# The top-k threshold of three batches found bit by bit with sign passes, in place of rounds of the eight largest

## The chip, the core and the metric

The kernel runs on one NeuronCore of a Trainium2 chip. The metric is the device time of one execution, in microseconds (us). Engines are named as the profile names them: PE is the matrix engine (its weight loads stand apart as PEld), DVE the vector engine, ACT the scalar engine, POOL the GpSimd engine, SP the engine that issues most DMAs. Each engine works through its own queue in order, and an instruction may wait for semaphores that other instructions, of other engines or of its own, count up.

## The reference, cut to what matters

The model has four steps, each added to the residual `x` (4 batches of 512 tokens of 512 numbers): a learned adjacency, a quantized feed-forward with Hadamard transforms, a 16-head cross attention over latent context, and a second quantized feed-forward. Only the first is changed:

```python
x = x + tanh(g_xattn[0]) * adjacency(ctx_512, layernorm(x), Wq, Wk, gamma_raw)

def adjacency(h, adj_raw, Wq, Wk, gamma_raw):       # h: 4 x 512 x 128
    ...                                             # Q, K: four heads of h @ Wq.T, h @ Wk.T
    sim = einsum('bhnd,bhmd->bnm', Q, K) / (sqrt(32.0) * 4)       # 4 x 512 x 512
    k = 153                                         # 0.3 of 512
    threshold = top_k(sim, k)[0][:, :, -1:]         # of each row: its 153rd largest
    A = sigmoid(sim) * (sim >= threshold)
    A = (A + swapaxes(A, -1, -2)) * 0.5
    gamma = sigmoid(gamma_raw)
    return (1 - gamma) * adj_raw + gamma * A
```

So each of the 512 rows of similarities of a batch needs its own threshold, the 153rd largest of its 512 numbers.

## The kernel before, in words

**Tiles.** The 512 rows of a batch lie as NT = 4 tiles of 128 partitions by 512 numbers, all in fp32. `adjacency(b)` projects the context (PE, tile `pq`), forms the similarities of each tile with one matmul into PSUM (`psim`, line 475) and copies them scaled to SBUF with ACT (`sim`, line 477). Then come `rounds` = 20 rounds for two tiles at a time: DVE's MAX8 finds the eight largest of each row (`m`, line 486), and MATCH_REPLACE8 overwrites these eight with -3e38 in a work tile (`work`, line 491; the hardware runs it as a short MATCH_VALUE_LOAD and the pass itself). After round 20 the wanted number is the first of the last eight. A pass of DVE (line 497) then keeps the sigmoid (ACT, line 496) where the similarity is at least this threshold. Transposes on PE (`padj`) and three passes on DVE add it to `x`. For batch 0 all this runs alone, at the start of the kernel.

**Staging.** For batches 1 to 3, the adjacency, then the keys of the attention (`keys(b)`), then the first feed-forward (`feed0`) of batch b are generators that run in the background of the attention of batch b-1. `attention` loops over 32 pairs of heads, eight for a batch, and over four steps j within a pair. In each step it emits the current pair's scores and the next pair's queries:

- `pqh` (line 804): queries by PE, copied by ACT (`qh`, line 809); `pb` (819): queries through the compressed weights; DVE multiplies by cosines and sines (`ro`, `rs`, lines 827 to 832); POOL adds (833); `pr` (790, 792), copied by ACT (`qr`, 850).
- `pss` (863, 866): scores by PE; DVE takes the negated maximum of a row (`nm`, 871); ACT computes the exponentials with their sum (`pp`, 874, with an ACTIVATION_READ_ACCUMULATOR behind each), DVE the reciprocal (`rsm`, 876), ACT the scaled probabilities (877).
- `ppt` (885): transposes by PE, copied by ACT (`pT`, 886).
- at the pair's end `pc` (893): attended context by PE, copied by ACT (`cxo`, 898); `po` (905): output projection; DVE adds it to `x` (910).

**What sets the order.** The loop at the end of the kernel calls `next` on the attention, then draws on a background generator as long as the costs that it has yielded lie under a budget: a budget of 230 is spread over the steps up to four before batch b's attention begins, and what is left then is emitted at once. A tile framework puts the instructions of each engine in order and sets the semaphores. The DVE rounds of the top-k carry a lowered priority (`high_priority(offset=-FILL)`), so they fill the queue behind the attention's own work. With other work in flight, `gate_t` hands out one of two 2 KB buffers, `front_t` one of three, and `big` one of three 8 KB buffers.

Of the kernel before, what the change touches and what calls it, by code (L numbers as in the profile page):

```python
# [9 lines left out]
F32 = mybir.dt.float32  # L10
BF = mybir.dt.bfloat16
AF = mybir.ActivationFunctionType
ALU = mybir.AluOpType
AX = mybir.AxisListType

P = 128
B, S, D = 4, 512, 512
NT = S // P
# [6 lines left out]
TOPK = max(1, int(S * 0.3))  # L25
SIM_SCALE = 1.0 / (math.sqrt(32.0) * 4.0)
EPS = 1e-5
MAGIC = 12582912.0
GONE = -3.0e38
U16 = mybir.dt.uint16  # L30
F8 = mybir.dt.float8e4


# [1 line left out]
def flamingo_kernel(  # L35
# [9 lines left out]
    nc = tc.nc  # L45

    const = ctx.enter_context(tc.tile_pool(name="const", bufs=1))
    small = ctx.enter_context(tc.tile_pool(name="small", bufs=4))
    xp = ctx.enter_context(tc.tile_pool(name="xp", bufs=8))
# [16 lines left out]
    alone = [True]  # L66
    turn_of = {"tr": 0, "big": 0, "front": 0}

    def mine(kind, every):
        turn_of[kind] += 1  # L70
        return not alone[0] or turn_of[kind] % every == 0

    def bg_ps(name):
        return psb.tile([P, 512], F32, tag="bg", name=name)

    def gate_ps(name):
        return mm_ps(name) if alone[0] else bg_ps(name)
# [6 lines left out]
    def two_k(tag, bufs, name):  # L84
        return bp.tile([P, 512], F32, tag=tag, name=name, bufs=bufs)

    def front_t(name):
        if mine("front", 2):
            return two_k("front", 3, name)
        return wp.tile([P, 512], F32, tag="pp", name=name, bufs=7)  # L90

    def gate_t(name):
        if alone[0]:
            return wp.tile([P, 512], F32, tag="ro", name=name, bufs=7)
        return two_k("gate", 2, name)

    def back_t(name):
        return two_k("back", 2, name)
# [3 lines left out]
    def big(name):  # L102
        place = lent.pop(0) if lent else None
        if place == "h":
            t = hp.tile([P, NC, S], F32, tag="hT", name=name, bufs=1)
            return t.rearrange("p c s -> p (c s)")
        if place == "t":
            t = wp.tile([P, NT, S], F32, tag="pT", name=name)
            return t.rearrange("p j s -> p (j s)")
        if place == "b":  # L110
            return bp.tile([P, FF], F32, tag="big", name=name, bufs=3)
        turn_of["big"] += 1
        if not alone[0] or turn_of["big"] % 5 in (1, 3, 0):
            return bp.tile([P, FF], F32, tag="big", name=name, bufs=3)
        t = wp.tile([P, NT, S], F32, tag="pT", name=name)
        return t.rearrange("p j s -> p (j s)")
# [56 lines left out]
    def ln_stats(tiles, name):  # L173

        k = len(tiles)
        st = small.tile([P, k, 6], F32, tag=f"ln_st{k}", name=f"st_{name}")
        mv = small.tile([P, k, 2], F32, tag=f"ln_mv{k}", name=f"mv_{name}")
        for j, t in enumerate(tiles):
            nc.vector.bn_stats(st[:, j, :], t)
            nc.vector.bn_aggr(mv[:, j, :], st[:, j, :])  # L180
        return mv, rsqrt_cols(mv[:, :, 1], k, name)
# [261 lines left out]
    xs = {}  # L443

    FILL = 800

    def adjacency(b):
        cT = front_t(f"cT_{b}")
        nc.sync.dma_start(cT, cxT[:, b * S : (b + 1) * S])
        proj = []  # L450
        for i in range(2):
            pq = bg_ps(f"pq_{b}_{i}")
            nc.tensor.matmul(pq, wqk[:, i, :], cT, start=True, stop=True)
            t = bp.tile([P, S], F32, tag=f"qk{i}", name=f"qk{i}_{b}")
            nc.scalar.copy(t, pq)
            proj.append(t)
        qT, kT = proj
        if alone[0]:
            adj = hp.tile([P, NT, S], F32, tag="hT", name=f"adj_{b}", bufs=1)
        else:  # L460
            adj = big(f"adj_{b}").rearrange("p (j s) -> p j s", j=NT)
        rounds = (TOPK + 7) // 8
        at = (TOPK - 1) % 8
        for two in range(0, NT, 2):
            if two == (0 if alone[0] else NT - 2):
                for k in range(NT):
                    t = xp.tile([P, D], F32, tag="x", name=f"x{b}_{k}")
                    nc.sync.dma_start(t, x[(b * NT + k) * P : (b * NT + k + 1) * P, :])
                    xs[b, k] = t
            pair = range(two, two + 2)  # L470
            sims, works, m8 = {}, {}, {}
            for j in pair:
                i = f"{b}_{j}"
                psim = bg_ps(f"psim_{i}")
                nc.tensor.matmul(psim, qT[:, j * P : (j + 1) * P], kT, start=True, stop=True)
                sims[j] = gate_t(f"sim_{i}")
                nc.scalar.activation(sims[j], psim, AF.Copy, scale=SIM_SCALE)
                works[j] = back_t(f"work_{i}")


            cur = dict(sims)
            for r in range(rounds):
                with tc.high_priority(offset=-FILL):
                    for j in pair:
                        m8[j] = small.tile([P, 8], F32, tag="m8", name=f"m8_{b}_{j}_{r}")
                        nc.vector.max(m8[j], cur[j])  # L486
                yield 1.3
                with tc.high_priority(offset=-FILL):
                    if r < rounds - 1:
                        for j in pair:  # L490
                            nc.vector.match_replace(works[j], m8[j], cur[j], GONE)  # L491
                            cur[j] = works[j]
                yield 1.4
            for j in pair:
                sg = front_t(f"sig_{b}_{j}")
                nc.scalar.activation(sg, sims[j], AF.Sigmoid)
                nc.vector.scalar_tensor_tensor(
                    adj[:, j, :], sims[j], m8[j][:, at : at + 1], sg, ALU.is_ge, ALU.mult
                )
        mv, r = ln_stats([xs[b, j] for j in range(NT)], f"a{b}")  # L500

        kr = small.tile([P, NT], F32, tag="ckr", name=f"ckr_{b}")
        nc.vector.tensor_scalar(kr, r, c_keep, None, ALU.mult)
        km = small.tile([P, NT], F32, tag="ckm", name=f"ckm_{b}")
        nc.vector.scalar_tensor_tensor(km, mv[:, :, 0], -1.0, kr, ALU.mult, ALU.mult)
        nc.vector.tensor_scalar(kr, kr, 1.0, None, ALU.add)
        yield 5.0
        for j in range(NT):
            i = f"{b}_{j}"
            pt = gate_ps(f"padj_{i}").rearrange("p (k q) -> p k q", k=NT)  # L510
            for k in range(NT):
                nc.tensor.transpose(pt[:, k, :], adj[:, k, j * P : (j + 1) * P], ident)
            if alone[0]:
                nc.scalar.activation(
                    xs[b, j], xs[b, j], AF.Identity, bias=km[:, j : j + 1], scale=kr[:, j : j + 1]
                )
            else:
                nc.vector.tensor_scalar(
                    xs[b, j], xs[b, j], kr[:, j : j + 1], km[:, j : j + 1], ALU.mult, ALU.add
                )  # L520
            sym = front_t(f"sym_{i}")
            nc.vector.tensor_tensor(sym, adj[:, j, :], pt.rearrange("p k q -> p (k q)"), ALU.add)
            nc.vector.scalar_tensor_tensor(
                xs[b, j], sym, c_new, xs[b, j], ALU.mult, ALU.add
            )
            yield 2.0
# [433 lines left out]
    def step(gen, parts):  # L960
        for _ in range(parts):
            next(gen, None)

    a0, early, fw = adjacency(0), ahead(), feed_weights(True, "w0")
    step(early, 1)
    w0 = None
# [36 lines left out]
    def before(b):  # L1003
        k = keys(b)
        for n, cost in enumerate(adjacency(b)):
            yield cost
            if n % 6 == 5:

                with tc.high_priority(offset=-FILL // 4):
                    step(k, 1)  # L1010
        drain(k)
        yield from feed0(b, w0)
# [16 lines left out]
    for _ in attention(first):  # L1029
        done += 1  # L1030
        while job < len(jobs):
            gen, cost, until = jobs[job]
            start = jobs[job - 1][2] if job else 0
# [145 lines left out]
```

## Time and profile before

| what | value |
|---|---|
| time, median of 3 runs | 2048.83 us (2048.23 to 2052.68) |
| the profiled execution: time | 2048.82 us, all of it the span from the first to the last instruction |
| PE busy | 1819.6 us, 89% of the span |
| DVE busy | 1630.3 us, 80% |
| ACT busy | 1081.8 us, 53% |
| POOL busy | 336.1 us, 16% |
| MAX8, lines 486, all four batches | 320 instructions, 209.5 us of DVE |
| attention, first `pc` to last `po` | 312 us to 1961 us of the span |

The page gives, for each engine, the busy time, its course in 40 slices of 51 us, and groups of instructions with their mean duration and the idle time before them. Two instructions that follow each other on one engine overlap a little in the trace: the second starts before the first's end. So what an instruction takes of its engine is read from one start to the next start, and not from its duration. The stage of a background step can be read from windows of the trace that run from one pair's first `pc` matmul to the next pair's.

### The profile page before, as it was taken

How to read it: one execution, taken by the hardware profiler on the slowest of the kernel's cores; microseconds unless marked ns; L12 is line 12 of the kernel's file. 1: busy time of each engine (PE TensorE's matmuls, PEld its weight loads, DVE VectorE, ACT ScalarE, POOL GpSimd, SP SyncE). 2: the span in 40 equal slices, each digit the busy share in tenths (PEclk: the TensorE clock that was granted, in tenths of full speed). 3: DMA queues.
4: the chain of work that ended last, by engine and by line, in shares of the span. 5: the costliest groups of instructions: out<-in, count | busy, mean ns of one | idle time of the engine just before them, and what ended most of it. 6: DMA issues, size and time to landing. Idle time of an engine off the chain costs nothing. (4 is left out here: it accounts for less than half of the span.)

```text
span 2048.8 us, 22947 instructions
## 1 busy us (share of the span) xinstructions
PE 1819.6 (89%) x7874; PEld 889.2 (43%) x7874; DVE 1630.3 (80%) x3305; ACT 1081.8 (53%) x1833; POOL 336.1 (16%) x316
## 2 busy tenths in 40 slices
PE   1268799999999999999999999999989999999898
PEld 0035534436554344455444444555443444444333
DVE  7989699987776999977778999778758556866785
ACT  6935454354434455453444564534786565555544
POOL 3020031123011122130111221301111210111000
PEclk6579899999999999999999999999999999999999
DMA  7451021111111222111122121111783112222011
GB/s 269 155 179 38 1 74 45 55 49 28 42 43 48 89 71 72 38 38 37 41 55 84 57 84 47 35 35 38 241 302 128 50 40 74 68 53 67 21 34 39
DMA packets 115556, 151.90 MB, mean 74 GB/s; under 512 B 57456, under 2 KB 68080, under 8 KB 112368
## 3 DMA queue, kind: packets, MB, share of 16 engines
q1 hardware_dynamic: 109968, 134.51, 22.0%
q0 software_dynamic: 4320, 14.16, 1.9%
q10 hardware_dynamic: 1152, 1.77, 0.2%
q8 instruction: 62, 1.02, 0.2%
q14 instruction: 54, 0.44, 0.1%
HBM read 117.90 MB, written 19.92 MB: 67 GB/s over the span
## 5 line engine op out<-in xcount | busy, mean ns | idle before, releaser
L833 POOL TENSOR_TENSOR ro<-ro,rs 128x512 f32<-128x512 f32 x192 | 255.4, 1333 | 1153.3 <-DVE rs L829 648.3
L874 ACT ACTIVATE pp<-pss,nm 128x512 f32<-128x512 f32 x256 | 174.6, 685 | 272.3 <-DVE nm L871 271.5
L804 PE MATMUL pqh<-hT,wq 128*128 128x512 f32 x512 | 239.7, 606 | 6.8 <-ACT pp L874 5.6
L893 PE MATMUL pc<-pT,kv 128*128 128x512 f32 x512 | 236.0, 600 | 2.7 <-ACT pT L886 2.6
L905 PE MATMUL po<-om,cxo 128*128 128x512 f32 x512 | 229.9, 597 | 0.0
L819 PE MATMUL pb<-qh,wc 128*128 128x512 f32 x384 | 189.4, 613 | 13.6 <-ACT qh L809 7.7
L486 DVE MAX8 m<-work 128x8 f32<-128x512 f32 x304 | 198.7, 684 | 0.6
L871 DVE TENSOR_REDUCE nm<-pss 128x1 f32<-128x512 f32 x256 | 167.8, 683 | 38.1 <-PE pss L866 37.9
L491 DVE MATCH_REPLACE8 work<-m,work 128x512 f32<-128x512 f32 x288 | 193.6, 678 | 0.1
L877 ACT ACTIVATE pp<-pp,rsm 128x512 f32<-128x512 f32 x256 | 178.6, 720 | 27.4 <-DVE rsm L876 26.2
L886 ACT COPY pT<-ppt 128x512 f32<-128x512 f32 x256 | 142.1, 588 | 38.5 <-PE ppt L885 38.0
L885 PEld LDWEIGHTS ppt<-ident,pp 128*128 128x128 f32 x1024 | 117.7, 142 | 96.6 <-issue 37.1
L885 PE MATMUL ppt<-ident,pp 128*128 128x128 f32 x1024 | 147.8, 279 | 10.1 <-ACT pp L877 4.4
L910 DVE SCALAR_TENSOR_TENSOR x<-po,gt,x 128x512 f32<-128x512 f32 x128 | 94.8, 745 | 68.4 <-PE po L905 67.6
L804 PEld LDWEIGHTS pqh<-hT,wq 128*128 128x128 f32 x512 | 93.1, 191 | 128.4 <-issue 89.6
L863 PE MATMUL pss<-kr,qr 64*128 64x512 f32 x256 | 143.4, 641 | 4.4 <-ACT pp L874 2.6
L905 PEld LDWEIGHTS po<-om,cxo 128*128 128x128 f32 x512 | 93.9, 190 | 119.5 <-issue 101.2
L866 PE MATMUL pss<-kr,qr 64*128 64x512 f32 x256 | 143.4, 641 | 0.7 <-DVE ro L827 0.5
L827 DVE TENSOR_TENSOR ro<-pb,cos_q 128x512 f32<-128x512 f32 x192 | 130.9, 682 | 10.3 <-PE pb L819 9.5
L893 PEld LDWEIGHTS pc<-pT,kv 128*128 128x128 f32 x512 | 91.9, 190 | 105.0 <-issue 90.4
L819 PEld LDWEIGHTS pb<-qh,wc 128*128 128x128 f32 x384 | 65.6, 189 | 113.6 <-issue 40.9
L898 ACT COPY cxo<-pc 128x512 f32<-128x512 f32 x64 | 37.4, 584 | 145.1 <-PE pc L893 144.8
(279 smaller groups left out, 3062.0 us busy)
## 6 DMA issues: line engine op xcount, KB each, us to landing
wq<-in_wqh SPq DMA_DIRECT2D x64, 256.0 KB, 2.7
om<-omd SPq DMA_DIRECT2D x64, 256.0 KB, 2.8
wc<-in_wkcq SPq DMA_DIRECT2D x32, 384.0 KB, 3.1
krd<-krs POOLq DMA_DIRECT2D x32, 256.0 KB, 2.5
kr<-krd SPq DMA_DIRECT2D x32, 256.0 KB, 2.7
sa_w1v<-in_gvT SPq DMA_DIRECT2D x8, 1024.0 KB, 5.3
sb_w1v<-in_gvT SPq DMA_DIRECT2D x8, 1024.0 KB, 5.2
wr<-in_wqr SPq DMA_DIRECT2D x32, 192.0 KB, 2.4
```

The lines of the kernel that those rows point to most:

```text
L486: nc.vector.max(m8[j], cur[j])
L491: nc.vector.match_replace(works[j], m8[j], cur[j], GONE)
L804: nc.tensor.matmul(pq, self.wqs[i][:, c, :], hT[self.b][:, c, :], start=(c == 0), stop=(c == NC - 1),)
L819: nc.tensor.matmul(pb, self.wc[:, at : at + P], self.qhs[i if i < 2 else o], start=True, stop=True)
L833: nc.gpsimd.tensor_tensor(ro, ro, rs, ALU.add)
L863: nc.tensor.matmul(*args, start=True, stop=True)
L871: nc.vector.tensor_reduce(nm, pss[i], AX.X, ALU.max, negate=True)
L874: nc.scalar.activation(pp, pss[i], AF.Exp, bias=nm, accum_out=sm)
L877: nc.scalar.activation(pp, pp, AF.Copy, scale=rs)
L885: nc.tensor.transpose(pt[:, l, :], pp[:, l * P : (l + 1) * P], ident)
L893: nc.tensor.matmul(pc, kv[self.b][:, l, :], self.pT[i][:, l, :], start=(l == 0), stop=(l == NT - 1),)
L905: nc.tensor.matmul(po, self.cxo[i][:, j * P : (j + 1) * P], self.oms[i], start=(i == 0), stop=(i == 1),)
```

## The change

For batches 1 to 3 the rounds go. All four similarity tiles are copied to the 8 KB buffer `adj` first; then `kth` finds the 153rd largest of each row. It settles one bit of the fp32 pattern at a time: a first pass finds the sign of the wanted number, and each of 31 further steps tests a candidate. The count of the numbers above the candidate comes from ACT: a Sign activation of `sig * sim + test` with a running sum along the row, one pass for each of the four tiles, into one column of `cnt` each. The sign tiles themselves go to one scratch buffer, `junk`. Then three DVE operations on 128 x 4 numbers compare the counts with `need` and set and clear bits of `test`. At the end some small DVE operations and one counting pass of DVE for each tile settle the last bit. Sigmoid and masking stay as they were. Batch 0 keeps its rounds.

```diff
+    def kth(b, sims):
+        st = small.tile([P, 8, NT], F32, tag="kth", name=f"kth_{b}", bufs=1)
+        cnt, sig, need, test, r, u, hi, lo = (st[:, k, :] for k in range(8))
+        ints = lambda t: t.bitcast(I32)
+        junk = gate_t(f"signs_{b}")
+
+        def signs(**how):
+            for j in range(NT):
+                col = slice(j, j + 1)
+                nc.scalar.activation(
+                    junk, sims[:, j, :], AF.Sign, accum_out=cnt[:, col],
+                    **{k: v[:, col] for k, v in how.items()},
+                )
+
+        nc.vector.memset(test, -2.0)
+        signs()
+        nc.vector.tensor_scalar(sig, cnt, float(2 * TOPK - S), 2.0, ALU.is_ge, ALU.mult)
+        nc.vector.tensor_scalar(sig, sig, 1.0, None, ALU.subtract)
+        nc.vector.tensor_scalar(need, sig, float(2 * TOPK - S - 1), 1.0, ALU.mult, ALU.add)
+        yield 3.4
+        for bit in range(30, -1, -1):
+            signs(scale=sig, bias=test)
+            nc.vector.tensor_tensor(ints(r), cnt, need, ALU.is_lt)
+            if bit:
+                nc.vector.tensor_scalar(
+                    ints(r), ints(r), bit, 1 << (bit - 1), ALU.logical_shift_left, ALU.bitwise_or
+                )
+            nc.vector.tensor_tensor(ints(test), ints(test), ints(r), ALU.bitwise_xor)
+            yield 3.4
...
+        for j in range(NT):
+            nc.vector.tensor_scalar(
+                junk, sims[:, j, :], hi[:, j : j + 1], 0.0, ALU.is_ge, ALU.add,
+                accum_out=cnt[:, j : j + 1],
+            )
+        nc.vector.tensor_scalar(ints(u), cnt, float(TOPK), None, ALU.is_ge)
+        nc.vector.copy_predicated(lo, ints(u), hi)
+        yield 5.0
+        return lo
+
     def adjacency(b):
...
+        if not alone[0]:
+            for j in range(NT):
+                psim = bg_ps(f"psim_{b}_{j}")
+                nc.tensor.matmul(psim, qT[:, j * P : (j + 1) * P], kT, start=True, stop=True)
+                nc.scalar.activation(adj[:, j, :], psim, AF.Copy, scale=SIM_SCALE)
+                yield 1.0
+            limit = yield from kth(b, adj)
+            tokens()
+            for j in range(NT):
+                sg = front_t(f"sig_{b}_{j}")
+                nc.scalar.activation(sg, adj[:, j, :], AF.Sigmoid)
+                nc.vector.scalar_tensor_tensor(
+                    adj[:, j, :], adj[:, j, :], limit[:, j : j + 1], sg, ALU.is_ge, ALU.mult
+                )
-        for two in range(0, NT, 2):
+        for two in range(0, NT if alone[0] else 0, 2):
...
```

`tokens()` is the loading of the batch's four tiles of `x`, which stood between the two pairs of tiles before and now follows `kth`. The sign passes have no lowered priority.

More of the change, by code (lines that the diff above doesn't have):

```diff
@@ L29 @@
 GONE = -3.0e38
-U16 = mybir.dt.uint16
+I32 = mybir.dt.int32
 F8 = mybir.dt.float8e4
@@ L445, in flamingo_kernel @@
     FILL = 800
+    def kth(b, sims):
[25 more added lines that the diff above has]
+            yield 3.4
+        nc.vector.tensor_scalar(ints(test), ints(test), 0x7FFFFFFF, None, ALU.bitwise_and)
+        nc.vector.memset(ints(u), 1)
+        nc.vector.tensor_tensor(ints(r), ints(test), ints(u), ALU.add)
+        nc.vector.tensor_scalar(ints(u), sig, 0.0, None, ALU.is_gt)
+        nc.vector.tensor_copy(hi, test)
+        nc.vector.tensor_copy(lo, r)
+        nc.vector.copy_predicated(hi, ints(u), r)
+        nc.vector.copy_predicated(lo, ints(u), test)
+        nc.vector.tensor_tensor(hi, hi, sig, ALU.mult)
+        nc.vector.tensor_tensor(lo, lo, sig, ALU.mult)
+        for j in range(NT):
[7 more added lines that the diff above has]
+        return lo
     def adjacency(b):
@@ L463, in adjacency, with tokens @@
         at = (TOPK - 1) % 8
-        for two in range(0, NT, 2):
[L465 to L469, printed above, removed]
+        def tokens():
+            for k in range(NT):
+                t = xp.tile([P, D], F32, tag="x", name=f"x{b}_{k}")
+                nc.sync.dma_start(t, x[(b * NT + k) * P : (b * NT + k + 1) * P, :])
+                xs[b, k] = t
+        if not alone[0]:
[13 more added lines that the diff above has]
+        for two in range(0, NT if alone[0] else 0, 2):
+            if two == 0:
+                tokens()
             pair = range(two, two + 2)
```

## The prediction

> **What bounds the kernel now.** I read the page first: its busy times, then its slices.
>
> ```profile
> PE 1819.6 (89%) x7874; PEld 889.2 (43%) x7874; DVE 1630.3 (80%) x3305; ACT 1081.8 (53%) x1833; POOL 336.1 (16%) x316
> ...
> PE   1268799999999999999999999999989999999898
> PEld 0035534436554344455444444555443444444333
> DVE  7989699987776999977778999778758556866785
> ACT  6935454354434455453444564534786565555544
> ```
>
> From the fifth slice on PE is nearly full; DVE reaches nines in three stretches, where the rounds of batches 1 to 3 run. So I cut windows from one pair's first `pc` to the next's: two pairs with rounds, then two without.
>
> ```profile
> 352.20:392.20 40.00, 39.01 (x124) 16.48 (x122) 38.72 (x85) 19.41 (x41) 8.06 (x7) 1.00 0.16 49
> 817.70:858.50 40.80, 38.48 (x122) 16.56 (x123) 39.95 (x87) 18.74 (x38) 7.61 (x6) 1.00 0.16 47
> ...
> 1565.90:1605.30 39.40, 38.27 (x121) 16.24 (x121) 33.41 (x80) 26.47 (x44) 7.62 (x6) 1.00 0.23 71
> 1605.30:1644.70 39.40, 38.66 (x134) 16.96 (x132) 19.73 (x37) 19.03 (x40) 7.93 (x6) 1.00 0.17 49
> ```
>
> Columns: length, then busy time of PE, PEld, DVE, ACT, POOL, then the granted clock (full). With 40 us of DVE work a pair takes 40 to 41 us; with 20 us it takes 39.4. PE sets the pair; the full DVE adds a microsecond. Over ten pairs with rounds (40 to 46 us; the longer ones hold more PE work) PE idles 1.9 us per pair, in the two free ones 0.9. The room for a gain is that microsecond, times some twelve pairs. ACT has 19 of 40 us of work.
>
> The Trainium skill, "Perfetto Trace Analysis", section "Identifying the Most-Contended Engine", calls matmul busy time a bad measure of headroom and takes LDWEIGHTS busy instead. That is 42% here, and by it PE has room and DVE is the bound; the last window above, with DVE half idle and no faster, speaks against it. By the page rival 1 below could bring more than 15 us; the forecast would stay as it is, since ACT's queue ends the pair either way.
>
> **What goes.** 240 MAX8 and 228 MATCH_REPLACE8 (three quarters of these rows, batch 0 staying):
>
> ```profile
> L486 DVE MAX8 m<-work 128x8 f32<-128x512 f32 x304 | 198.7, 684 | 0.6
> L491 DVE MATCH_REPLACE8 work<-m,work 128x512 f32<-128x512 f32 x288 | 193.6, 678 | 0.1
> ```
>
> 240 x 0.684 + 228 x 0.678 = 319 us of DVE. By the windows this is worth 12 x (1.9 - 0.9) = 12 us of the end, hardly more.
>
> **What comes.** 384 Sign passes, 128 per batch; none was in the trace in this form. What ACT pays is read from start to start:
>
> ```profile
> 1621.18 0.69 ACT L874 ACTIVATE pp<-pss,nm 128x512 f32<-128x512 f32 x1 [8.14 <-DVE nm L871]
> 1621.77 0.19 ACT L874 ACTIVATION_READ_ACCUMULATOR pp<-pss,nm 128x1 f32 x1
> 1621.86 0.68 ACT L874 ACTIVATE pp<-pss,nm 128x512 f32<-128x512 f32 x1
> ...
> 1622.52 1.33 ACT L877 ACTIVATE pp<-pp,rsm 128x512 f32<-128x512 f32 x2
> ```
> ```profile
> 51.48 0.80 ACT L514 ACTIVATE x<-x,ckm,ckr 128x512 f32<-128x512 f32 x1
> 52.18 1.90 ACT L239 ACTIVATE ja_w0u<-sa_w0u 128x2048 bf16<-128x2048 f32 x1
> ```
>
> A running sum costs an extra read instruction, and the exponential with it takes 0.59 + 0.09 = 0.68 us. L514 is the same shape with both scale and bias from SBUF, as the Sign has: 0.70 to the next start. So a pass is 0.70 + 0.09 = 0.79 us; bounds 0.68 (the exponential) and 0.92. The upper one is for passes in a row: all write the scratch tile `junk`, and in the built order each waits for the one before to finish. The trace has one such wait, where the next activation starts 0.22 us after the read instead of 0.09:
>
> ```profile
> 31.36 0.18 ACT L239 ACTIVATION_READ_ACCUMULATOR ja_w0g<-sa_w0g 128x1 f32 x1
> 31.58 1.91 ACT L239 ACTIVATE ja_w0u<-sa_w0u 128x2048 bf16<-128x2048 f32 x1
> ```
>
> Between two bits stands a round trip through DVE: three dependent small operations at 0.2 us from start to start, plus 0.03 us each way.
>
> ```profile
> 1065.16 0.16 DVE L167 TENSOR_TENSOR t_q<-r_q 128x4 f32<-128x4 f32 x1
> 1065.36 0.16 DVE L168 TENSOR_TENSOR t_q<-t_q,w_q 128x4 f32<-128x4 f32 x1
> 1065.55 0.17 DVE L169 TENSOR_SCALAR t_q<-t_q 128x4 f32<-128x4 f32 x1
> ```
>
> That is 0.65 us on a free DVE, and one DVE pass (0.6 us from start to start) more when it queues behind `ro`, `rs` or `nm`, so 0.65 to 1.25. What is queued behind a sign that waits so on ACT: the exponentials, scalings and copies of the attention, and behind those PE.
>
> **One pair after.** In the built order the signs of a batch fall on some four pairs: nine pairs carry 27 to 32 signs each, five carry 5 to 25, and 28 signs come before the first pair. A full pair's ACT queue:
>
> - attention: 8 exponentials x 0.68, 8 scalings x 0.61 (two take 1.33 above), 13 copies x 0.49 (`pT` lasts 0.59 and overlaps the next by 0.1) = 16.7 us;
> - 31 signs x 0.79 = 24.5;
> - 11 of them directly behind a sign, 0.13 more each: 1.4;
> - eight bits: two round trips fully bare (2 x 0.65 = 1.3), as signs of two bits follow each other behind the last `cxo`; the other six have one attention operation (0.5 to 0.7 us) in between and cost about 0.3 each, 1.8;
> - a copy of keys or a table load: 0.8.
>
> Sum 46.5 us, against 39.0 of PE work (the windows' 38.3 to 39.0, and in batches 2 and 3 a matmul of the keys or two). ACT becomes the bound, and PE idles 7.5 us per pair where it idled 1.9.
>
> On the table loads: the built program has 109 where there were 102, since `sig` now stands among signs and exponentials; Sign itself runs under the table that is loaded. The trace has 1.28 us for one, 1.3 to the next start, so 7 x 1.3 = 9 us of ACT in all, inside the sum above. "ScalarE: Activation LUTs", section "What ACT_TABLE_LOAD costs", gives about 2.7 us for a switch, with a drain that no row here shows. By it the seven cost 19 us, and the forecast would rise by some 10.
>
> **The sum**, against the profiled execution, whose 2048.8 us are all span and equal the median:
>
> - nine full pairs x (7.5 - 1.9) = +50;
> - five part pairs (ACT about as long as PE): +1 each, +5;
> - the start, 250 to 312 us: ACT was busy 32 of 62 us and takes 28 signs more (+23 us), which fits, but single copies that PE waits for queue behind a sign: +2; DVE, 55 of 62 us busy, loses 24 us of rounds there: -2;
> - feed-forward: the built order ends the search about a pair later, and what follows must still be out before the next batch's `hidden_T`. Bounds 0 to 10 us per batch (10 us is one step j, a quarter of a pair); I take 2: +6.
> - hidden at nothing: 279 small DVE operations and the last counting passes (DVE has become the emptier engine), the later loads of `x` (needed a stage later), the scratch buffer.
>
> +61: 2048.8 + 61 = 2110 us.
>
> **Rivals.**
>
> 1. ACT keeps up, the DVE stretches open: -12 from the pairs and -3 at the start, 2034 us. It decides once a sign costs under (39.4 - 16.7 - 0.8) / 31 = 0.71 us with its read and its share of the round trips. For: 20 us of ACT are idle per pair. Against: the exponential alone takes 0.68, with one pointer and no wait. Chance 0.06. Within 0.2% (about what a measurement can tell from no change): 0.04, between this and the next.
> 2. Cheap signs at 0.68 with all waits as above: pair 43.1 us, nine x (4.1 - 1.9) = +20, with the rest +31: 2080. Chance 0.12.
> 3. The round trips are not covered, each bit stalling ACT for 1.25 us (DVE's three operations are apart in its queue, with `ro` and `rs` between them that wait for PE): 8 x 1.25 = 10 us per pair instead of 3.1, 9 x 6.9 = +62 on top: 2172. Chance 0.12.
> 4. The squeezed feed-forward makes PE wait before each next batch's queries, the full 10 us three times: 2134. For: its transposes by DMA are in the chain that ended last. Against: the attention's own matmuls cover part. Chance 0.08.
>
> That the search isn't done as said is no rival: the built program has all 384 passes and none of the 468.
>
> **How the numbers follow.** The forecast itself holds 0.58, from 2085 to 2130. The range, 2060 to 2168, takes in rivals 2 and 4 and leaves out 1, no change and most of 3 (0.06 + 0.04 + 0.1 = 0.2). Faster 0.06, same 0.04, slower 0.90.
>
> **What would show it.** Right: signs of 0.80 us with reads of 0.19; full pairs of 45 to 48 us with ACT busy over 40 of them, PE's idle time ended by ACT's `qh`, `pp` and `pT`; DVE near 20 us per pair; the chain of waits with more ACT in it. Pairs of 40 us, or ACT idle in them, would prove it wrong; a pair over 50 points to rival 3, idle PE around `phT` to rival 4.

## The result, and the profile after

The changed kernel takes 2161.61 us (median of 4 runs, 2156.61 to 2163.79), the kernel before on the same chip 2050.76 us (2048.23 to 2053.5). The ratio is 1.0538, with a 95% interval from 1.052 to 1.0556: 111 us slower. The forecast was 2110 us. Its sign and its bound were right and its size was not, so the experiments ask two things: whether ACT's queue is the bound, and where the other 50 us come from. Of the run without search below, one execution, the profiled one, ran at a granted clock of 0.55 and took 3131 us; its median is that of the other three, and it has no windows.

The page of the changed kernel: busy times, then the slices of PE, DVE and ACT.

```profile
PE 1852.7 (86%) x7874; PEld 897.8 (42%) x7874; DVE 1426.1 (66%) x2957; ACT 1397.8 (65%) x2608; POOL 337.7 (16%) x316
...
PE   1277888889998888889989888899979999999898
...
DVE  6989454457876554567774544777756747686685
ACT  6935689985443899844448899454468556565544
```

DVE's busy time fell by 204 us and ACT's rose by 316. PE does the same 7874 matmuls. Its row of nines now has eights in most slices where the signs run, and there ACT has eights and nines. Two things add up to the loss: PE's idle time (span less busy) went from 229.2 to 308.0 us, +78.8, and PE's busy time from 1819.6 to 1852.7, +33.1. The forecast held only the first.

The price of a pass, in the groups of ACT's instructions:

```profile
L461 ACT ACTIVATE signs<-adj,kth 128x512 f32<-128x512 f32 x372 | 302.2, 812 | 28.6 <-DVE kth L479 18.3 <-DVE rsm L949 6.0 <-DVE kth L469 1.2
L461 ACT ACTIVATION_READ_ACCUMULATOR signs<-adj,kth 128x1 f32 x372 | 71.2, 191 | 0.0
```

And ACT's queue in the second pair of batch 1's search, in order of time:

```profile
374.21 0.81 ACT L461 ACTIVATE signs<-adj,kth 128x512 f32<-128x512 f32 x1
...
375.14 0.81 ACT L461 ACTIVATE signs<-adj,kth 128x512 f32<-128x512 f32 x1
...
377.68 0.81 ACT L461 ACTIVATE signs<-adj,kth 128x512 f32<-128x512 f32 x1 [0.69 <-DVE kth L479]
...
381.03 0.80 ACT L461 ACTIVATE signs<-adj,kth 128x512 f32<-128x512 f32 x1
...
381.83 0.71 ACT L950 ACTIVATE pp<-pp,rsm 128x512 f32<-128x512 f32 x1
```

Two signs in a row stand 0.93 us apart (374.21 to 375.14): the second waits until the first has left `junk`. With the attention's work next (381.03 to 381.83) a sign takes 0.80. A round trip that nothing covers idles ACT for 0.69 us. These are the forecast's prices (0.92, 0.79, 0.65).

Windows from pair to pair, columns as in the prediction, with DMA share and GB/s at the end: one pair each of batch 1's, 2's and 3's search, with 31 signs in each, and one without search.

```profile
362.73:409.70 46.97, 41.10 (x121) 17.14 (x121) 21.73 (x58) 43.34 (x102) 7.63 (x6) 0.97 0.14 41
...
728.01:774.40 46.39, 40.75 (x124) 17.30 (x124) 25.74 (x64) 43.22 (x101) 7.62 (x6) 1.00 0.28 90
1226.18:1276.42 50.24, 42.24 (x124) 17.49 (x123) 24.41 (x58) 43.55 (x102) 8.70 (x8) 0.97 0.16 50
1638.12:1677.62 39.50, 37.95 (x122) 16.25 (x120) 21.77 (x45) 29.39 (x48) 7.59 (x6) 1.00 0.81 288
```

These three take 46 to 50 us, with ACT busy for 43 of them and DVE for 22 to 26; without the search it is 39.5 us, as before. All nine full pairs, with 28 to 32 signs, take 43.7 to 51.6 us. What PE waited for in the first three of them (total, times, longest):

```profile
PE ppt L958 <- ACT pT L959: 6.2, 10, 0.8
...
PE ppt L958 <- ACT pp L950: 2.6, 2, 1.3
PE pb L892 <- ACT qh L882: 2.6, 4, 0.9
```

Copies and scalings that ACT has queued behind signs come first, as forecast (POOL's `ro`, 4.5 us, stands between these lines).

### The profile page after: what moved, and what is told of

It is laid out like the page before. It is cut to its first block, busy times and chain, and to the rows that moved or that the text cites. A ratio compares the mean times of both kernels' runs of the same rounds, so it can differ in the third digit from the quotient of the medians.

```text
span 2160.7 us, 23544 instructions
## 1 busy us (share of the span) xinstructions
PE 1852.7 (86%) x7874; PEld 897.8 (42%) x7874; DVE 1426.1 (66%) x2957; ACT 1397.8 (65%) x2608; POOL 337.7 (16%) x316
## 3 DMA queue, kind: packets, MB, share of 16 engines
q1 hardware_dynamic: 109968, 134.51, 20.6%
## 5 line engine op out<-in xcount | busy, mean ns | idle before, releaser
L461 ACT ACTIVATE signs<-adj,kth 128x512 f32<-128x512 f32 x372 | 302.2, 812 | 28.6 <-DVE kth L479 18.3
L892 PE MATMUL pb<-qh,wc 128*128 128x512 f32 x384 | 194.6, 625 | 21.6 <-ACT qh L882 17.2
L958 PE MATMUL ppt<-ident,pp 128*128 128x128 f32 x1024 | 157.6, 288 | 36.5 <-ACT pT L959 23.9
L863 PE MATMUL pr<-ro,wr 128*64 128x512 f32 x192 | 102.3, 632 | 44.1 <-POOL ro L906 35.2
L474 DVE TENSOR_TENSOR kth<-kth 128x4 int32<-128x4 f32 x93 | 21.4, 230 | 179.0 <-ACT signs L461 178.8
```

Of the source, the lines that this page charges most:

```text
L461: nc.scalar.activation(junk, sims[:, j, :], AF.Sign, accum_out=cnt[:, col], **{k: v[:, col] for k, v in how.items()},)
L892: nc.tensor.matmul(pb, self.wc[:, at : at + P], self.qhs[i if i < 2 else o], start=True, stop=True)
L958: nc.tensor.transpose(pt[:, l, :], pp[:, l * P : (l + 1) * P], ident)
```

## The experiments

The table takes every run together; the windows and idle times are those of each kernel's profiled execution. "Full" are the ten pairs that hold the search in the changed kernel (numbers 0 to 2, 7 to 10 and 15 to 17 from the first `pc`), "other" the other thirteen pairs up to the 23rd, which hold the part searches and the feed-forward. The same numbers are used in every row; in a kernel whose search is shorter or lies elsewhere, some of the ten hold few signs or none. Idle is the idle time ahead of PE's matmuls. "Clock" is the sum over these 23 windows of (1 - PEclk) x length: the full-speed time that the granted clock withheld, also while PE was idle.

| kernel | median us | ratio to before (95%) | full pair: mean us | ACT busy in it | PE idle, full | PE idle, other | clock |
|---|---|---|---|---|---|---|---|
| before | 2050.8 | 1 | 42.6 | 21.4 | 19.9 | 49.4 | 10.2 |
| changed | 2161.6 | 1.0538 (1.052 to 1.0556) | 47.5 | 43.6 | 62.4 | 84.7 | 37.6 |
| no search | 2064.8 | 1.0064 (1.0048 to 1.0081) | | | | | |
| no round trips | 2152.9 | 1.0499 (1.0481 to 1.0517) | 47.6 | 44.7 | 52.7 | 73.3 | 49.4 |
| denser search | 2178.2 | 1.0622 (1.0606 to 1.0638) | 48.8 | 44.7 | 62.7 | 89.4 | 45.3 |
| before, rounds later | 2070.6 | 1.0096 (1.0079 to 1.0113) | 42.0 | 20.9 | 19.5 | 64.9 | 23.9 |
| half search | 2075.4 | 1.0122 (1.0107 to 1.0137) | 42.8 | 33.0 | 26.4 | 62.2 | 10.6 |
| two scratch tiles | 2188.5 | 1.0672 (1.0656 to 1.0688) | 49.4 | 43.1 | 70.6 | 83.8 | 76.2 |
| ACT and DVE | 2103.4 | 1.0265 (1.0248 to 1.0282) | 44.0 | 33.4 | 36.6 | 72.5 | 21.1 |
| low priority | 2178.7 | 1.062 (1.0595 to 1.0645) | 42.0 | 38.1 | 31.8 | 143.4 | 62.6 |
| half search, earlier | 2075.7 | 1.0114 (1.0092 to 1.0136) | 43.7 | 33.6 | 29.4 | 57.5 | 13.0 |
| before, rounds earlier | 2074.0 | 1.0107 (1.0092 to 1.0122) | 43.7 | 21.9 | 22.5 | 57.2 | 20.6 |
| ACT and DVE, low priority | 2113.5 | 1.0299 (1.0282 to 1.0316) | 44.7 | 33.8 | 42.3 | 65.9 | 26.6 |
| 24 bits | 2117.5 | 1.0348 (1.032 to 1.0375) | 46.0 | 40.2 | 47.3 | 64.6 | 27.6 |

### No search at all, and no round trips

```diff
-            limit = yield from kth(b, adj)
+            limit = small.tile([P, NT], F32, tag="kth", name=f"kth_{b}", bufs=1)
+            nc.vector.memset(limit, 0.05)
+            for n in range(32):
+                yield 3.4
+            yield 5.0
```

> The changed kernel with the search left out (no sign passes, no bit updates; the threshold is a constant), at the same places and with the same yielded costs. If the sign passes in ACT's queue are the whole loss, it falls below the kernel before, by the room that the page showed: 2034 to 2045 us, 0.98 to 1.00 of before. If the late feed-forward (drawn by the same costs) carries a part of its own, that part stays: 2060 to 2080 us.

Measured: 2064.84 us, still 14 us over the kernel before, though 319 us of DVE's rounds are gone and nothing took their place. So 97 of the 111 us are the search on ACT. The other 14 go with the rest of the change; that they come from where the generator's order now puts the other steps is likely from the shifted runs below, but not seen in a trace of this run.

In the second run the passes stay and the three DVE operations of each bit go from the loop:

```diff
         for bit in range(30, -1, -1):
             signs(scale=sig, bias=test)
-            nc.vector.tensor_tensor(ints(r), cnt, need, ALU.is_lt)
-            ...
-            nc.vector.tensor_tensor(ints(test), ints(test), ints(r), ALU.bitwise_xor)
             yield 3.4
+        nc.vector.tensor_tensor(ints(r), cnt, need, ALU.is_lt)
```

> All 384 sign passes, but always at the first candidate: the three small DVE operations after each bit are left out, so no pass waits for DVE. If ACT's time for the passes is the loss, little changes: the bare round trips are 2 of 46.5 us a pair, so some 2135 to 2155 us. If the round trips are the loss, most of the 111 us goes: under 2100 us.

Measured: 2152.86 us. Without any round trip the kernel gains 9 us. PE's idle time over the whole span falls by more, from 308.0 to 285.8 us, but its busy time grows from 1852.7 to 1862.3, and the clock withholds 12 us more. The passes also moved closer together: eight of the ten pairs now hold 32 to 36 signs each, and these eight take 45.5 to 50.2 us. Rival 3 of the prediction, 62 us for the round trips, is out: the passes themselves are most of the loss.

### Denser, and the kernel before with a later search

```diff
-        yield 3.4        # after the first pass, and after each bit
+        yield 2.4
```

> The costs that the search yields go from 3.4 to 2.4 per bit, so that it is drawn over fewer attention steps and the feed-forward begins about a pair earlier. If the loss is ACT's time alone, the same work is only denser: 2155 to 2170 us. If the squeezed feed-forward carries about 10 us per batch: 2125 to 2140 us.

Measured: 2178.19 us, 17 us more than the changed kernel. The edit did less than was meant: 297 signs stand in the ten full pairs, where 294 stood, and the feed-forward of batch 1 (its first `pn_f`) begins at 495.8 us in place of 501.5. So the run doesn't settle what a feed-forward a pair earlier would bring. It shows that another order of the same passes costs 17 us: the full pairs take 48.8 us, and the clock withholds 8 us more.

```diff
-                yield 1.3        # the kernel before, after MAX8
+                yield 1.42
-                yield 1.4        # after MATCH_REPLACE8
+                yield 1.525
```

> The kernel before, with its rounds, but with yielded costs of 2.945 in place of 2.7 per round, so that its search is drawn as late as in the changed kernel. If lateness by itself costs some 10 us per batch: 2070 to 2085 us. If it costs nothing without the sign passes: 2045 to 2056 us, 1.00 of before.

Measured: 2070.57 us, 20 us more than before, with no sign pass in it. The loss isn't in the pairs with rounds (42.0 us, before 42.6) but in the others. The largest single piece stands in pair 22, before batch 3's feed-forward must be done:

```profile
PE phT L761 <- DVE nq L184: 9.5, 1, 9.5
```

In the kernel before this wait was 3.3 us; in the changed kernel it is 9.2. The clock took part too: it withheld 23.9 us in place of 10.2.

### Half of the bits

```diff
-        for bit in range(30, -1, -1):
+        for bit in range(30, -1, -2):
...
-            yield 3.4
+            yield 6.6
```

> Leaves out every second bit of the search (16 bits in place of 31, 204 sign passes in place of 384), with the cost that one bit has in the generator's order raised from 3.4 to 6.6, so that the search is spread over the same pairs (its threshold is a coarser one). Queue theory (a full pair is the longer of ACT's queue and PE's work): a full pair's ACT queue falls from 46.5 by half of its 25 us of signs to 34 us, under PE's 39, so the pair is set by PE again and only the late feed-forward and some bare round trips stay: 2070 to 2085 us, full pairs of 40 to 42 us. Rival, each pass costs PE its share wherever it stands (it delays the evictions that PE waits for): the 97 us between the run without search (2064.9) and the changed kernel (2161.6) fall to 17/32 of it, 51 us: 2116 us, full pairs of 43 to 44 us.

Measured: 2075.42 us, as the queue theory said; the rival's 2116 is far off. One of its full pairs, with 24 signs:

```profile
315.89:357.33 41.44, 38.86 (x120) 16.73 (x121) 20.76 (x52) 37.16 (x85) 7.64 (x6) 1.00 0.14 46
```

With 37 us of work on ACT, PE's 39 us set the pair again, but for 2 us, and the clock is full. The passes were not thinned out evenly, though: the trace has 16 to 24 of them in each of eight pairs, and few or none in the rest. The 204 passes cost 10 us against the run without search; the other 180 cost 86. ACT's load acts as a threshold and not as an even toll on each pass.

### Without the wait on the scratch tile

```diff
-        junk = gate_t(f"signs_{b}")
+        junks = [gate_t(f"signs_{b}_{k}") for k in range(2)]
+        junk = junks[0]
...
-                    junk, sims[:, j, :], AF.Sign, accum_out=cnt[:, col],
+                    junks[j % 2], sims[:, j, :], AF.Sign, accum_out=cnt[:, col],
```

> The four sign passes of a bit write two scratch tiles in turn in place of one, so that a pass no longer waits for the end of the pass before it. In a row, passes stood 0.94 us apart in the changed kernel and 0.81 apart with other work between. If this wait of 0.13 us is paid by two of three passes in the nine full pairs (31 passes in each): 9 x 20 x 0.13 = 24 us less, 2138 us, and full pairs of 44 to 45 us. If other work stands between most passes anyway, a third of this or less: 2153 to 2162 us. The rival that ACT's load does not set the pair: no change, 2158 to 2165 us.

Measured: 2188.49 us, 27 us slower than the changed kernel, outside all that was expected. The wait did go. ACT's queue, in order of time:

```profile
325.40 0.83 ACT L462 ACTIVATE signs<-adj,kth 128x512 f32<-128x512 f32 x1
...
326.21 0.82 ACT L462 ACTIVATE signs<-adj,kth 128x512 f32<-128x512 f32 x1
...
327.00 0.82 ACT L462 ACTIVATE signs<-adj,kth 128x512 f32<-128x512 f32 x1
...
327.80 0.82 ACT L462 ACTIVATE signs<-adj,kth 128x512 f32<-128x512 f32 x1
```

Four signs stand 0.80 us apart. But they now stand in one block. In the changed kernel's trace 259 of the 384 signs have other work on both sides; here 65 have, and 52 blocks hold four. Why is seen only from the two orders: with the wait on `junk` the framework put an eviction between two signs, and without it, it does not. Now an eviction waits for a block of 3.2 us, and PE for the eviction. What PE waited for in two full pairs, and the window of the first:

```profile
PE ppt L959 <- ACT pT L960: 10.7, 4, 4.2
PE pc L967 <- ACT pT L960: 6.5, 3, 2.2
```
```profile
324.60:379.15 54.55, 43.73 (x121) 19.61 (x121) 23.36 (x62) 49.65 (x114) 7.63 (x6) 0.84 0.11 35
```

The clock in it is 0.84. Of the 27 us, 19 stand in the ten full pairs and 9 before the first pair. In the full pairs PE's idle time grew by only 8 us, while the clock withheld 46.2 us in place of 12.6, so much of the price of the longer waits is paid in the clock. A shorter queue with longer blocks in it was worse than a longer one that is interleaved.

### Half of the counting on DVE

```diff
-            signs(scale=sig, bias=test)
+            signs(range(HA), scale=sig, bias=test)      # HA = 2
+            counts(range(HA, NT))      # DVE: sims * sig > test, summed along the row
```

> Of the four tiles of a batch two are still counted by ACT's signs and two by DVE (a comparison with a running sum, on a copy of the tile turned by its sign), bit by bit as before. Queue theory: ACT's queue in a full pair falls to about 34 us, DVE's busy time rises from 22 by some 15 passes of 0.75 to 33 us, both under PE's 39 to 41: full pairs of 40 to 42 us, 2070 to 2085 us. Rival, each pass delays the eviction or the normalisation behind it on whichever engine it stands: 384 passes as before, so 2130 to 2165 us. Second rival, the batch's late threshold alone is left: 2065 us, as without search.

Measured: 2103.42 us. ACT's load in a full pair falls to 33.4 us and 58 us come back, but the time is 18 us above the expected range. One of the first two pairs, both of 45 us, in which neither ACT nor DVE is full:

```profile
311.09:356.00 44.91, 40.02 (x120) 16.76 (x120) 38.38 (x105) 35.53 (x80) 7.62 (x6) 0.96 0.13 42
```

A bit now ends when both engines are done; in the first two pairs ACT idled 9.5 us before signs for DVE's update, and DVE 7.0 us for ACT's counts.

### Low priority for the passes

```diff
-            signs(scale=sig, bias=test)
-            nc.vector.tensor_tensor(ints(r), cnt, need, ALU.is_lt)
+            with tc.high_priority(offset=-FILL):
+                signs(scale=sig, bias=test)
+            with tc.high_priority(offset=-FILL):
+                nc.vector.tensor_tensor(ints(r), cnt, need, ALU.is_lt)
...
```

> The sign passes and the updates of a bit are given a lower priority in the scheduler's order (by the length of the filling), so that an eviction or a softmax step of the attention that is ready stands ahead of them on ACT. If ACT's load sets the full pairs, nothing is gained: 2155 to 2170 us, full pairs of 46 to 48 us. Rival, the passes cost time because they stand ahead of steps that PE waits for: full pairs of 42 to 43 us, 2110 to 2130 us. If the threshold comes later by this, its feed-forward loses up to 15 us more: 2175 us.

Measured: 2178.71 us. The pairs do what the rival said, the time does what the last sentence said. One of the pairs, and the one in which the feed-forward was finished:

```profile
354.43:396.48 42.05, 38.23 (x123) 16.24 (x122) 21.88 (x52) 37.86 (x86) 7.64 (x6) 1.00 0.15 46
604.31:746.60 142.29, 100.12 (x583) 57.12 (x583) 82.25 (x130) 55.98 (x112) 9.93 (x9) 0.87 0.13 32
```

Pairs of 42 us and a full clock, with 24 signs in each where there were 30: the signs take only what ACT has left. But so the search lasts a pair or two longer, into the fifth pair of batch 1's time and the sixth of batch 2's, and the feed-forward has no attention left to hide under. PE's longest wait in the second window:

```profile
PE pd_f L436 <- DMA zT_f<-q_f: 32.6, 4, 15.1
```

So ACT's spare time is what is short: some 24 signs fit in a pair, and the fifth and sixth pair are needed for the feed-forward.

### Whether it is lateness

```diff
-            yield 6.6        # the half search
+            yield 5.8
```

> The half search again (204 sign passes), with its cost in the generator's order cut from 6.6 to 5.8 a bit, so that adjacency as a whole has the cost that it has in the kernel before (121 in place of 134). If the 14 to 20 us that the run without search and the kernel before with later rounds lost come from this lateness, and the half search itself is hidden: 2055 to 2062 us. Rival, the order loses by any shift of the steps, in whichever direction: 2070 to 2085 us again. If the signs, now 14% denser, make full pairs ACT-bound: pairs over 43 us and 2080 us or more.

```diff
-                yield 1.3        # the kernel before, after MAX8
+                yield 1.18
-                yield 1.4        # after MATCH_REPLACE8
+                yield 1.275
```

> The kernel before with its rounds put 9% earlier in the generator's order (1.18 and 1.275 in place of 1.3 and 1.4), the mirror image of the run with later rounds, which lost 20 us. If lateness costs in proportion: 2030 to 2040 us, unless DVE, whose rounds then stand denser in a pair (40 us of 40 already), becomes the bound: 2060 us. Rival, the loss comes from single steps that fall in or out of place with the pairs: anything from 2040 to 2070 us, with the gains and losses in single pairs of the feed-forward.

Measured: 2075.68 us and 2073.98 us. Giving the half search's adjacency the total cost that it had before changes nothing, and the kernel before loses 22 us also when its rounds come earlier. So lateness alone is not what costs: the steps of the kernel before stand well with its own costs, and each of the three shifts tried without any sign lost 14 to 22 us (no search, later, earlier). The shifts are small, though. The feed-forward of batch 1 (its first `pn_f`) begins 41% into the fourth pair in the kernel before, 42% and 44% in the kernels with later and earlier rounds, and 81% in the changed kernel, so a shift as large as that one was not tried without signs. In the run with earlier rounds the largest piece is another one, in the sixth pair, where the exponentials stood late on ACT:

```profile
PE pqh L804 <- ACT pp L874: 6.3, 1, 6.3
```

### Both engines, at low priority

```diff
-            signs(range(HA), scale=sig, bias=test)      # in the run with ACT and DVE
-            counts(range(HA, NT))
+            with tc.high_priority(offset=-FILL):
+                signs(range(HA), scale=sig, bias=test)
+                counts(range(HA, NT))
+            with tc.high_priority(offset=-FILL):
...                                                      # the updates, as above
```

> Two tiles counted by ACT's signs and two by DVE, as in the earlier run of 2103 us, and in addition the passes and updates get the low priority that the rounds of the kernel before had. With all four tiles on ACT the low priority brought the pairs with signs to 42.0 us, but the search went on into the next batch's time, and PE waited 58 us for the feed-forward's transposes. With half of the signs the search should end by the fourth pair, so that the pairs of 45 us become 42: nine x 3 = 27 us less, 2076 us. Rival, the search ends later also here and the feed-forward is late: 2100 us or more, with PE waiting for pd_f's transposes. Second rival, the round trips through DVE set the pace (ACT waited 9.5 us for them in two pairs): no change, 2095 to 2110 us.

Measured: 2113.5 us, 10 us more than without. Pairs of 44.7 us, and ACT idled 12.2 us before signs for DVE's updates in the first two pairs: at low priority the updates come later in DVE's queue, and a bit takes the longer round trip. The second rival held. Of the versions with signs that settle every bit the one with ACT and DVE at plain priority is the best; none beats the kernel before.

### Where the threshold lies

```diff
-        for bit in range(30, -1, -1):
+        for bit in range(30, 6, -1):
...
-            yield 3.4
+            yield 4.4
```

> Leaves out the last seven bits of the search (300 sign passes in place of 384; the threshold is coarser), with the cost of a bit raised from 3.4 to 4.4, so that adjacency as a whole has the cost of the changed kernel. Between the half search (204 passes, 2075 us) and the whole one (384, 2161 us) it tells whether the cost of the passes sets in where ACT's queue passes PE's work, or grows with each pass. Queue theory: 27 signs per full pair become 21, ACT's queue 16.7 + 21 x 0.85 + 3 = 38 us, still under PE's 39 to 40: pairs of 41 to 43 us, 2080 to 2095 us. Rival, a cost per pass: 2075 + 86 x 96/180 = 2121 us, pairs of 44 to 45 us.

Measured: 2117.51 us, near the rival's number. But the pairs were not thinned out as expected: the search ended earlier, and the nine pairs that hold most of it have 20 to 31 signs, 27 on average where 21 were expected and the changed kernel has 30. So the run doesn't test an even load between the two. One of its pairs, with 27 signs:

```profile
753.16:797.20 44.04, 40.39 (x124) 17.02 (x125) 22.58 (x55) 40.54 (x94) 8.73 (x8) 1.00 0.19 59
```

Averaged over all passes, from 204 to 300 a pass costs (2117.5 - 2075.4) / 96 = 0.44 us, from 300 to 384 it costs 0.53, below 204 only 0.05. Pair by pair, the traces have eleven pairs with 24 signs (half searches and low priority), 40.8 to 42.4 us long; three with 27 (here), 42.7 to 44.0; and the nine of the changed kernel with 28 to 32, 43.7 to 51.6. So the knee lies near 24 signs in a pair. I had put the threshold where ACT's queue reaches PE's work. It lies earlier: the pair above is 3.5 us longer than ACT's busy time and than PE's. ACT itself waits within a pair: in the first three full pairs of the changed kernel it idled 4.6 us before signs for DVE's updates and 3.1 us before `cxo` for PE's `pc`.

## Why the prediction was right in sign and short by 50 us

**Right: the bound and the prices.** A sign costs 0.80 us, 0.93 in a row, a bare round trip 0.69; there are 109 table loads of 1.283 us, as the built program had it. The full pair was forecast at 46.5 us with PE idle for 7.5 of them; it takes 47.5 with 6.2 idle. The term "nine full pairs, +50" measured +49 in length (ten pairs: 475.3 against 426.1 us). That the two are so close is partly luck: PE's idle time gave 42.5 of the 49, and the rest is longer matmuls, which the term didn't have. The half search and the run without search bear out the mechanism: with 24 passes or fewer in a pair 86 us came back, without passes 97. The 50 us that the forecast lacks lie in the thirteen other pairs: they grew by 62 us (846.8 against 785.2), 35 of idle time and 26 of longer PE work, where the sum had +5 for the part pairs and +6 for the feed-forward.

**Too small: the feed-forward, +6.** This term failed twice. Its size: PE's idle time outside the full pairs grew from 49.4 to 84.7 us, +35. Its reason: I costed lateness, and the run with earlier rounds shows that a shift in either direction loses. The shifted kernels without signs or with half of them have 57.2 to 64.9 us there, so 8 to 15 of the 35 come with a small shift. The other 20 or so come on top with the whole search: the run with 24 bits has 64.6 us. But its feed-forward of batch 1 also begins earlier (47% into the fourth pair, the changed kernel's 81%), so whether the 20 us are the signs' or the later feed-forward's stays open. Which steps fall badly differs from run to run (`phT` in pair 22, `pqh` in the sixth pair), and no run here took one of them away by itself. The wait that grew most over the span is that of `pr` for POOL's sum of `ro` and `rs`, which comes at the end of the chain `qh`, `pb`, `ro` and `rs`. The same row in the kernel before, the changed kernel and the kernel before with later rounds (total, times, longest):

```profile
PE pr L790 <- POOL ro L833: 10.0, 13, 1.3
PE pr L863 <- POOL ro L906: 35.2, 26, 2.7
PE pr L790 <- POOL ro L833: 24.0, 17, 3.2
```

More than half of this growth is there without a single sign. The prediction didn't have this wait among its signs.

**Left out: PE's clock, some +22.** The sum took PE's work per pair as fixed. But the clock withheld 10.2 us of full speed before and 37.6 after. Part of that fell in idle time: PE's busy time at half clock in the 23 windows was 17.2 us before and 61.6 after. If work at half clock takes twice as long, half of the difference, 22 us, is the clock's part of the 33.1 us that PE's busy time grew; this is an estimate. In the traces the granted clock changes only from one step of 3.413 us to another. Five such steps of the changed kernel, at the end of one full pair and the beginning of the next (the clock is the third column from the right):

```profile
399.64:403.05 3.41, 2.95 (x17) 1.34 (x15) 3.32 (x7) 3.41 (x10) 1.28 (x1) 1.00 0.47 154
403.05:406.47 3.42, 2.13 (x12) 1.03 (x12) 1.17 (x5) 2.98 (x7) 1.27 (x1) 1.00 0.00 0
406.47:409.88 3.41, 1.58 (x11) 1.01 (x10) 0.49 (x3) 3.41 (x10) 0.00 (x0) 1.00 0.19 58
409.88:413.29 3.41, 3.41 (x5) 1.35 (x6) 0.00 (x0) 3.34 (x9) 0.00 (x0) 0.50 0.01 2
413.29:416.71 3.42, 3.42 (x10) 1.51 (x9) 0.49 (x3) 2.35 (x6) 0.00 (x0) 1.00 0.00 0
```

In the third step PE is busy for 1.58 of 3.41 us, 46%; the next step is granted half the clock, and its dense work goes at half speed (5 matmuls, where the full step behind it has 10). The thirteen profiles with windows above, from 300 us on, hold 6591 steps at full clock that another step follows. After all 130 of them with PE busy for less than 43% the clock was halved, after 6313 of the 6323 with 55% or more it stayed full, and between these it was halved after 40 of 138. So idle time of PE was paid for twice in places: in the full pairs the clock withheld 12.6 us, where the kernel before lost none. It isn't idle time alone that decides, but how it gathers in a step: with two scratch tiles, where the full pairs lost 46 us of clock to 71 us idle, PE's share falls to 24% in a step of the first two pairs; with low priority, where they lost none to 32, no step of the first four pairs is under 61%. What the clock is worth in time was not tested by itself, and it is not one to one: four executions of the kernel with two scratch tiles had a mean clock of 0.930 to 0.952 over the span, and their times lie within 5 us.

The Trainium skill, "TensorE: Matmul & The Clock Gate", section "HAM oscillation — how this bites in real kernels", gives as a rule no idle gaps of PE beyond about 3.4 us. Here the clock halved after a step in which PE was 46% busy and no gap was over 0.7 us; the measurement decides, and the rule is too lenient for this kernel.

**Too large: the round trips.** The sum had 3.1 us in each of nine pairs, 28 us; taking them all away gained 9 us of time, though 22 us of PE's idle time over the span: the rest went into PE's busy time, and the signs moved closer together, so the run doesn't give the term alone. In the changed kernel ACT idled 18.3 us before signs for the updates in all (the row of the signs above); most of what one round trip delays, other work on ACT fills.

**The rivals.** Rival 1 and rival 2 fell with the price of a sign. Rival 3 named a time near the measured one (2172 us) and was wrong: the round trips are mostly covered. Its sign, a pair over 50 us, is there twice, in batch 3 (51.6 and 50.2 us), but ACT waited only 3.5 us for updates in these two pairs together. Rival 4's sign, PE idle around `phT`, is there once, 9.2 us in pair 22, and it stands in the kernel before with later rounds as well. The Trainium skill's measure of headroom from "Perfetto Trace Analysis", section "Identifying the Most-Contended Engine", went from 43% (the prediction has 42%) to 42% of the span while the kernel lost 111 us; the windows had it right.

Together, in PE's terms: +42.5 idle in the full pairs, +35.3 in the others, +1 elsewhere, and +33.1 of longer busy time, of which some 22 by the clock: 111.9 us between the two profiled executions.

## What to carry to other kernels

Work that moves from one engine to another must be set against the spare time of the engine that takes it, pair by pair: ACT held some 24 passes in a pair for 2 us, and beyond the half search each pass cost about half a microsecond on average. Here ACT held up the others before it was full: pairs with 24 passes were some 2 to 4 us longer than ACT's busy time, so such room has to be left. In this kernel with its tuned order, each change of a background step's cost first cost the tuning (14 to 22 us, in both directions), so test a change with the work taken out and the order left, and look in the trace whether the steps moved as meant.

## What the runs showed of the hardware that was not expected

- PE's granted clock changed only between steps of 3.413 us. It went to 0.50 for one step after a step in which PE was 46% busy, though no gap in it was over 0.7 us; under 43% it was halved every time (130 steps), at 55% or more hardly ever (10 of 6323).
- A wait of an instruction on its own engine, 0.13 us here, can be worth more than it costs: without it 52 blocks of four passes formed, and the kernel lost 27 us.
- A Sign with neither scale nor bias from SBUF (the first passes, 12 of them) has a mean of 638 ns, with both it has 812.
